# Two small share operations of each expert tile, moved from VectorE to GpSimd

## The chip, the cores and the metric

The kernel runs on one core of one Trainium2 chip. A core has five engines with a queue of instructions each: TensorE (PE; its weight loads are shown as PEld), VectorE (DVE), ScalarE (ACT), GpSimd (POOL), and SyncE (SP), which here only issues DMAs. The engines run side by side and wait for each other by semaphores. The metric is the device time of one execution in microseconds; the lower the better.

## The reference

The input x has 2 batches of 2048 rows of 256. Each row is layer-normalised, and two results are added to it. One is a selective scan along the rows of a batch, taken in an order sorted by cluster. The other is a mixture of 8 experts, of which each row uses its best two:

```python
x = L0_attn_x
xn = _layernorm(x, axis=-1)
x = x + _L0_attn_ref(xn, ...) + _L0_ffn_ref(xn, ...)
...
logits = xt @ w_gate
top_logits, sel = jax.lax.top_k(logits, TOP_K)
probs = jax.nn.softmax(top_logits, axis=-1)
h = jax.nn.silu(xt @ w1[e]) * (xt @ w3[e])
y = h @ w2[e]
out = sum over the two experts of y * probs
```

(The last four lines are written here per expert; the reference computes every expert for every row and then picks.) The share that the change is about is `probs`: the weight with which an expert's result enters a row.

## The kernel before

**The front** (to about 85 us) normalises the rows, chooses clusters and experts, sorts, and writes the normalised rows to DRAM (`xn`). A row there has 256 + 4 numbers. The four behind the row are: the index of its first expert (less 8, column D), the share of its second expert (D+1), the difference of the first share and the second (D+2), and the index of its second expert.

**The expert tiles.** Rows are grouped by expert into 71 tiles of 128 rows; a tile has one expert. `token_of` lists each tile's rows, `w_row` the rows of its weights, `te8` the index of its expert (less 8). A tile t goes through `part_up(t, 0)`, `part_up(t, 1)` and `part_down(t)`:

- `load_rows` (L830): GpSimd gathers the 128 rows from `xn` by an indirect DMA into `xg_sb` (4 buffers).
- `turn` (L839 to L847): TensorE transposes the rows, ScalarE copies them to `xT`, and the two small operations find `own`, one number for each row: (first expert == this tile's expert) x difference + second share. That is the row's share in this tile. `own` has 6 buffers.
- `up` (L856): 32 matmuls by w1 or w3 into PSUM; ScalarE's tanh (L864), VectorE's `silu` (L869) and `gate` (L873).
- `down` (L879): 8 matmuls by w2; ScalarE scales the rows by `own` as it copies them from PSUM into `yo` (L883, 3 buffers); GpSimd adds them to `acc` in DRAM by an indirect DMA (L797), behind the adds before.
- `load_up`, `load_down` (L816): GpSimd fetches the weights of tile t + 3 into the buffers (3 of each) that tile t has just left. Where tile t + 3 has the same expert as tile t, the indices are out of bounds and nothing is moved.

`turn_tile(t)` calls `turn` and then `load_rows` of tile t + 3. It is called in `part_down(t - 2)`, that is two tiles before `own` is used. So in GpSimd's queue a tile's turn of the wheel is: fetch w1/w3, gather rows, add rows, fetch w2.

**The scan** runs in 8 pieces of 512 places, each in 8 steps of four VectorE scans: ScalarE makes `da` (L741), VectorE makes `bu` (L747) and scans `hs` (L756), TensorE transposes `hs` (L768), ScalarE copies to `ht` (L772) and TensorE contracts over the states (L777). GpSimd gathers a piece's rows (`xs`, L601) and adds its results to `acc` (`yt`, L797), four transfers of each per piece.

**The order.** Each engine executes in the order of the text: the last lines of the kernel chain every instruction behind the one before on its engine. The order itself is made when the program is built. Scan steps are laid out place by place, and a job of an expert tile is put in as soon as the sum of the TensorE work given so far falls behind a fixed ratio of VectorE's, by estimates in the code (`PART = 2.05` and `PART_DVE = 0.5` us for a job). These estimates are not touched by the change, so every other instruction keeps its place among those of its engine.

Of the kernel before, what the change touches and what calls it, by code (L numbers as in the profile page):

```python
# [62 lines left out]
def scan_moe_kernel(  # L63
# [14 lines left out]
    nc = tc.nc  # L78
    B, L, D = x.shape
# [527 lines left out]
    class Piece:  # L607
# [9 lines left out]
        def turn(self, h: int):  # L617
            if h == 0:
                self.u = pre.tile([P, ND, CH], F32, tag="tok", name="u")
            pt = ps_m.tile([P, JC, P], F32, tag="m", name="pt_u")  # L620
            for i in range(JC):
                nc.tensor.transpose(pt[:, i, :], self.xs[:, i, h * P : (h + 1) * P], ident)  # L622
            nc.scalar.copy(self.u[:, h, :], pt.rearrange("p i t -> p (i t)"))
# [187 lines left out]
    class Tile:  # L811
# [23 lines left out]
        def turn(self):  # L835
            xg = self.xg
            pt = ps_m.tile([P, ND, P], F32, tag="m", name="pt_g")
            for h in range(ND):
                nc.tensor.transpose(pt[:, h, :], xg[:, h * P : (h + 1) * P], ident)  # L839
            self.xT = ffn.tile([P, ND, TS], F32, tag="xT", name="xT")  # L840
            nc.scalar.copy(self.xT, pt)
            self.own = ffn.tile([P, 1], F32, tag="own", name="own", bufs=6)
            nc.vector.scalar_tensor_tensor(
                self.own, xg[:, D : D + 1], te8[:, self.t : self.t + 1], xg[:, D + 2 : D + 3],
                ALU.is_equal, ALU.mult,
            )
            nc.vector.tensor_add(self.own, self.own, xg[:, D + 1 : D + 2])  # L847

        def up(self, i: int):
            wk = w13_sb[self.t % NW][:, i * ND * H : (i + 1) * ND * H].rearrange(  # L850
# [299 lines left out]
```

## Time and profile before

| what | us |
|---|---|
| median of 3 runs | 818.54 (816.89 to 818.64) |
| the profiled execution | 815.95 |
| its span | 814.1 |
| VectorE busy | 713.9 |
| GpSimd busy | 516.4 |
| ScalarE busy | 504.0 |
| GpSimd's instructions in the span | 374 |

The span is the time from the first to the last profiled instruction. A group row of the profile gives line, engine, operation, what is written <- what is read, shapes and count, then busy us and mean ns, then the idle time of the engine just before these instructions and what ended most of it. A timeline row gives start, duration, and the idle time before in brackets. In the slices each digit is the busy share in tenths of one fortieth of the span (20.4 us).

### The profile page before, as it was taken

The page shows a single profiled execution, that of the slowest core. Times are in us where ns is not written, and L with a number is a line of the kernel's source. Part 1 is how long each engine was busy: PE and PEld are TensorE (multiplying, and loading weights), DVE is VectorE, ACT ScalarE, POOL GpSimd, SP SyncE. Part 2 cuts the span into 40 slices and gives each one's busy share as a digit, 9 for nine tenths or more (in the row PEclk, how much of TensorE's full clock was granted, in tenths as well). Part 3 has the DMA queues.
Part 4 walks back from the last instruction along what each step waited for, and adds up shares of the span by engine and source line. Part 5 has one row for each costly group of instructions (what it writes and reads, how often), then busy time and mean ns, then how long its engine had stood idle before and what let it go on. Part 6 is the DMA issues. An engine that isn't in the chain of part 4 may idle for free.

```text
span 814.1 us, 17139 instructions
## 1 busy us (share of the span) xinstructions
PE 734.4 (90%) x6640; PEld 634.8 (78%) x6640; DVE 713.9 (88%) x1168; ACT 504.0 (62%) x976; POOL 516.4 (63%) x374
## 2 busy tenths in 40 slices
PE   8918697989999999989999999999999998999963
PEld 8914676869987898869877998698869895998842
DVE  8177528989999999989998999899999999799992
ACT  2432136649576866776669666865777667667572
POOL 2002463856786788757877886888758888777413
PEclk8555598999999999999999999999999999999996
DMA  8366343475246845663666458547654775443462
GB/s 266 117 233 187 111 101 129 116 254 154 49 127 171 266 104 167 170 219 86 170 176 204 106 163 253 134 104 234 192 130 99 228 226 119 98 99 95 92 213 26
DMA packets 61216, 125.91 MB, mean 155 GB/s; under 512 B 24464, under 2 KB 42032, under 8 KB 53776
## 3 DMA queue, kind: packets, MB, share of 16 engines
q0 software_dynamic: 40224, 65.03, 33.6%
q1 hardware_dynamic: 20912, 59.80, 21.6%
q8 instruction: 52, 0.85, 0.4%
q14 instruction: 28, 0.23, 0.1%
HBM read 180.06 MB, written 27.00 MB: 254 GB/s over the span
## 4 chain that ended last, share of the span: by engine, by line
PE 67%; ACT 6%; DVE 3%; DMA 2%; issue 2%; POOL 1%; POOLq 0%; SPq 0%; ACTq 0%; DVEq 0%
PE p_ps L856 28%; PE py L879 14%; PE pt_s L768 12%; PE y L777 6%; ACT ht L772 2%; DMA out_dram<-acc 2%; PE y L709 2%; PE pt_g L839 2%; PE px L636 1%; PE pd L673 1%; DVE hs L756 1%; ACT da L741 1%; DVE bu L747 1%; PE px L641 1%; PE pt_u L622 1%
## 5 line engine op out<-in xcount | busy, mean ns | idle before, releaser
L856 PE MATMUL p_ps<-xT,w 128*128 128x128 f32 x2272 | 282.8, 281 | 4.5 <-ACT sq L683 4.3
L856 PEld LDWEIGHTS p_ps<-xT,w 128*128 128x128 f32 x2272 | 271.1, 196 | 19.2 <-issue 9.7
L756 DVE TENSOR_TENSOR_SCAN hs<-da,carry,bu 128x512 f32<-128x512 f32 x192 | 246.3, 1283 | 0.0
L741 ACT ACTIVATE da<-dl,na 128x512 f32<-128x512 f32 x256 | 182.0, 723 | 1.1 <-DVE hs L756 1.0
L747 DVE TENSOR_TENSOR bu<-du,bt 128x512 f32<-128x512 f32 x256 | 174.1, 681 | 0.0
L797 POOL DMA_INDIRECT acc<-yo,token_of x71 | 132.8, 1870 | 64.9 <-ACT yo L883 22.1
L816 POOL DMA_INDIRECT w<-in_w_up_dram,w_row x71 | 93.1, 1312 | 113.6 <-DVE w_row L565 58.6
L772 ACT COPY ht<-pt_s 128x512 f32<-128x512 f32 x256 | 137.2, 590 | 31.4 <-PE pt_s L768 30.9
L768 PE MATMUL pt_s<-ident,hs 128*128 128x128 f32 x1024 | 138.3, 279 | 14.7 <-ACT ht L772 8.7
L879 PE MATMUL py<-w,g 128*128 128x256 f32 x568 | 138.7, 388 | 12.2 <-ACT r L677 8.7
L768 PEld LDWEIGHTS pt_s<-ident,hs 128*128 128x128 f32 x1024 | 118.0, 144 | 31.6 <-ACT ht L772 15.6
L879 PEld LDWEIGHTS py<-w,g 128*128 128x128 f32 x568 | 104.0, 193 | 27.1 <-ACT r L677 10.3
L830 POOL DMA_INDIRECT xg_sb<-xn,token_of x71 | 90.6, 1276 | 34.6 <-issue 15.2
L816 POOL DMA_INDIRECT w<-in_w_down_dram,w_row x71 | 94.2, 1327 | 21.6 <-issue 14.0
L864 ACT ACTIVATE t_sb<-p_ps 128x512 f32<-128x512 f32 x71 | 42.6, 600 | 72.1 <-PE p_ps L856 71.9
L883 ACT ACTIVATE yo<-py,own 128x256 f32<-128x256 f32 x71 | 33.9, 477 | 79.9 <-PE py L879 78.4
L756 DVE TENSOR_TENSOR_SCAN hs<-da,bu 128x512 f32<-128x512 f32 x64 | 78.2, 1222 | 0.0
L777 PE MATMUL y<-ht,z 128*32 128x128 f32 x2048 | 74.3, 279 | 2.6 <-ACT ht L772 1.9
L777 PEld LDWEIGHTS y<-ht,z 128*32 128x32 f32 x2048 | 51.1, 110 | 24.6 <-issue 13.5
L797 POOL DMA_INDIRECT acc<-yt,line_of x28 | 54.1, 1933 | 21.4 <-issue 6.7
L869 DVE SCALAR_TENSOR_TENSOR t_sb<-t_sb,p_ps 128x512 f32<-128x512 f32 x71 | 48.2, 679 | 10.4 <-ACT t_sb L864 10.1
L873 DVE SCALAR_TENSOR_TENSOR g<-t_sb,p_ps 128x512 f32<-128x512 f32 x71 | 48.3, 681 | 7.2 <-PE p_ps L856 4.3
(184 smaller groups left out, 679.2 us busy)
## 6 DMA issues: line engine op xcount, KB each, us to landing
bt<-bc SPq DMA_DIRECT2D x32, 1024.0 KB, 5.2
z<-bc SPq DMA_DIRECT2D x32, 256.0 KB, 3.7
xn<-xt SPq DMA_DIRECT2D x8, 520.0 KB, 4.9
xt<-in_x_dram SPq DMA_DIRECT2D x8, 512.0 KB, 7.2
acc<-in_x_dram SPq DMA_DIRECT2D x8, 512.0 KB, 6.5
w<-in_w_up_dram,w_row POOLq DMA_INDIRECT x71, 6.8
w<-in_w_down_dram,w_row POOLq DMA_INDIRECT x71, 3.8
xg_sb<-xn,token_of POOLq DMA_INDIRECT x71, 3.5
```

Of the source, the lines that this page charges most:

```text
L741: nc.scalar.activation(self.da[i], self.piece.dl[:, self.h, :], AF.Exp, scale=na[:, self.h, n : n + 1])
L747: nc.vector.tensor_mul(self.bu[i], self.piece.du[:, self.h, :], self.piece.bts[self.q][:, i, :])
L756: nc.vector.tensor_tensor_scan(self.hs[:, :, i], self.da[i], self.bu[i], start, ALU.mult, ALU.add)
L768: nc.tensor.transpose(pt[:, j, :], self.hs[:, t0 : t0 + G, :].rearrange("p t n -> p (t n)"), ident)
L772: nc.scalar.copy(self.ht[i], pt)
L777: nc.tensor.matmul(p.ys[self.h][j * G : (j + 1) * G, i, :], lhsT=p.zs[q][:, i * (P // G) + j, :], rhs=self.ht[i][:, j, :], start=False, st ...
L797: ins = nc.gpsimd.indirect_dma_start(out=to, out_offset=bass.IndirectOffsetOnAxis(ap=numbers, axis=0), in_=rows, in_offset=None, compute_o ...
L816: nc.gpsimd.indirect_dma_start(out=to[self.t % NW], out_offset=None, in_=rows, in_offset=bass.IndirectOffsetOnAxis(ap=w_row[:, self.t : se ...
L830: nc.gpsimd.indirect_dma_start(out=self.xg, out_offset=None, in_=xn_d, in_offset=bass.IndirectOffsetOnAxis(ap=token_of[:, self.t : self.t ...
L856: nc.tensor.matmul(p[:, f, :], lhsT=wk[:, h, f * P : (f + 1) * P], rhs=self.xT[:, h, :], start=h == 0, stop=h == ND - 1,)
L873: nc.vector.scalar_tensor_tensor(self.g, self.s, 0.5, self.p3, ALU.mult, ALU.mult)
L879: nc.tensor.matmul(py, lhsT=self.g[:, f, :], rhs=w2[:, f, :], start=f == 0, stop=f == NH - 1)
```

## The change

Both operations are given to GpSimd, as a tensor-by-scalar comparison and product and as an addition. They stand in GpSimd's queue where `turn` is called: after the fetch of w1/w3, ahead of the gather of tile t + 3. The arithmetic is the same.

```diff
             self.own = ffn.tile([P, 1], F32, tag="own", name="own", bufs=6)
-            nc.vector.scalar_tensor_tensor(
+            nc.gpsimd.tensor_scalar(
                 self.own, xg[:, D : D + 1], te8[:, self.t : self.t + 1], xg[:, D + 2 : D + 3],
                 ALU.is_equal, ALU.mult,
             )
-            nc.vector.tensor_add(self.own, self.own, xg[:, D + 1 : D + 2])
+            nc.gpsimd.tensor_add(self.own, self.own, xg[:, D + 1 : D + 2])
```

## The prediction

> **What bounds the kernel now.** I read the page's busy table first, then its slices, then the groups of GpSimd and VectorE in the stretch from 200 to 750 us, then the timeline.
>
> ```profile
> PE 734.4 (90%) x6640; PEld 634.8 (78%) x6640; DVE 713.9 (88%) x1168; ACT 504.0 (62%) x976; POOL 516.4 (63%) x374
> ...
> DVE  8177528989999999989998999899999999799992
> ...
> POOL 2002463856786788757877886888758888777413
> ...
> PE 67%; ACT 6%; DVE 3%; DMA 2%; issue 2%; POOL 1%; POOLq 0%; SPq 0%; ACTq 0%; DVEq 0%
> ```
>
> The chain is put down to TensorE (67%). But between 200 and 750 us, where 58 of the 71 expert tiles run beside the scan, VectorE's digits are 8 and 9, and the sum of its idle gaps there is 22 us of 550: it works back to back, and TensorE works nearly so. GpSimd looks free at 63%. It isn't, and this is the point of the forecast. Its groups from 200 to 750 us (columns: count, busy us and mean ns, then idle before and who ended it):
>
> ```profile
> L797 POOL DMA_INDIRECT acc<-yo,token_of x58 | 109.1, 1882 | 41.7 <-ACT yo L883 9.8 <-ACT da L741 6.2 <-ACT ht L772 5.2
> L816 POOL DMA_INDIRECT w<-in_w_down_dram,w_row x58 | 79.5, 1370 | 17.7 <-issue 11.0 <-PE pt_s L768 2.1 <-PE p_ps L856 1.8
> L816 POOL DMA_INDIRECT w<-in_w_up_dram,w_row x57 | 76.2, 1336 | 25.1 <-issue 7.3 <-PE p_ps L856 6.9 <-PE pt_g L839 5.7
> L830 POOL DMA_INDIRECT xg_sb<-xn,token_of x57 | 75.8, 1330 | 17.4 <-issue 12.2 <-DVE hs L756 1.8 <-DVE bu L747 1.5
> L797 POOL DMA_INDIRECT acc<-yt,line_of x26 | 49.6, 1909 | 20.8 <-issue 6.1 <-ACT ht L772 4.8 <-DMA acc<-yo,token_of 4.7
> L601 POOL DMA_INDIRECT xs<-xn,line_of x24 | 31.2, 1301 | 7.3 <-issue 6.4 <-DMA xs<-xn,line_of 0.6 <-DMA acc<-yo,token_of 0.3
> ```
>
> Busy: 109.1 + 79.5 + 76.2 + 75.8 + 49.6 + 31.2 = 421.4 us in 280 instructions. Idle: 130.0 us. But nearly every gap has a floor of 0.305 us ("issue 0.30" in the timeline, whatever the queue holds), so 280 x 0.305 = 85.4 us of that idle can't be used by another transfer. Real spare time is 130.0 - 85.4 = 44.6 us, or 44.6/57 = 0.78 us per tile. GpSimd is thus 92% taken, and it already runs late: from the timeline, the accumulating DMA of a tile (L797) starts a median 5.3 us and at worst 20.5 us after its rows are ready (L883). The last L856 matmul of a tile frees its up-weight buffer, and the refill (L816) starts a median 5.3 us later.
>
> **What the change removes.** Per tile, two VectorE instructions of 128x1:
>
> ```profile
> L843 DVE SCALAR_TENSOR_TENSOR own<-xg_sb,te 128x1 f32<-128x1 f32 x71 | 15.0, 211 | 0.0
> L847 DVE TENSOR_TENSOR own<-own,xg_sb 128x1 f32<-128x1 f32 x71 | 11.3, 160 | 2.4
> ```
>
> From the start of L843 to the start of what follows is 0.31 us (411.36 to 411.67 in the timeline), so VectorE gets back 71 x 0.31 = 22 us, 58 x 0.31 = 18 us of them in the stretch. TensorE is the other full engine: counted by the start-to-start spacing of each kind (0.11 us for a 128x128 L856 matmul), its matmuls fill some 93% of the stretch, so it can't follow all of that; I take 0.2 us a tile, two thirds, as the gain if nothing else changes: 58 x 0.2 = 12 us. Waits removed: the row gather (L830) waited for VectorE's "own" before it reused a buffer, 0.6 us in 2 places; nothing.
>
> **What it adds on GpSimd.** The order is load of up-weights, [own, own], gather of rows of tile t+3, accumulation of tile t-2, load of down-weights. No transfer is added or leaves its place; all four stand behind the pair. The first own waits for the gather of its rows: issued three tiles before, the time from issue to the transposes that need the same rows is 9.4 us at least (median 19) against a landing of 3.5 us, so that wait is over. (In the lead, tiles 0 and 1 do wait for it, about 3 us, where the queue stood still anyway: 4.3 us before the weight load at 99.6.) The second own waits for the first. ScalarE's yo (L883) now waits for GpSimd; the place where own will stand comes 6.2 us at least before yo (median 14.5), so nothing is late as long as GpSimd doesn't fall further back.
>
> The price of the pair has three terms, none of which the profile shows directly.
>
> (a) The instructions. Nearest rows:
>
> ```profile
> L208 POOL IOTA row_p<- 128x1 f32 x1 | 0.1, 142 | 0.0
> ...
> masks.py:66 POOL TENSOR_SCALAR_AFFINE_SELECT before<-before 128x128 f32<-128x128 f32 x1 | 0.3, 292 | 0.1
> ```
>
> A 128x1 write is 0.14 us; a read of 128 elements with a wait for the writer ahead is 0.29 us after a gap of 0.1. I take 0.2 for each own and 0.1 between: 0.5. Here a rule of the Trainium skill speaks: GPSIMD Engine Reference, "Engine selection", says that GpSimd takes about twice VectorE's time for two-input elementwise work. By it the pair would be 2 x (0.211 + 0.160) = 0.74. At 128x1 the elements hardly count, so I stay near the rows and keep 0.3 to 0.74.
>
> (b) The gaps. The pair puts one to two more hand-overs into the queue: 0 if small instructions follow each other as the iotas do (gap 0.0), 0.5 if each costs a transfer's 0.3. I take 0.15.
>
> (c) The shared port. The timeline around 409 us:
>
> ```profile
> 408.38 1.28 DVE L756 TENSOR_TENSOR_SCAN hs<-da,carry,bu 128x512 f32<-128x512 f32 x1
> 408.99 1.46 POOL L830 DMA_INDIRECT xg_sb<-xn,token_of  x1 [0.31 <-issue]
> 409.58 0.67 DVE L747 TENSOR_TENSOR bu<-du,bt 128x512 f32<-128x512 f32 x1
> ```
>
> This gather takes 1.46 us; beside a VectorE instruction that reads PSUM it takes 0.97 (207.29 us). Its end, 410.45, is 0.79 us after the scan's end at 409.66. All gathers and weight loads follow this: with "wait for the end of a VectorE instruction with two SBUF inputs that began earlier", the predicted excess differs from the recorded one by a median 0.034 us, and the mean excess is 0.36 us. So whatever reads SBUF on GpSimd pays 0.36 us at its turn. The skill's SBUF page (SBUF — State Buffer, "Who interferes with whom") states the same block for a VectorE instruction with two SBUF inputs, but infers that descriptor generation escapes it; the row shows that it doesn't. By the page's inference the transfers' excess would have another cause and the pair alone would wait; by the row both wait, and I put the pair through the recorded VectorE instructions: 0.35 us for the first own, 0.35 for the second (it comes out into the middle of the next one): 0.7 in all. From below: 0.4, if one wait serves both. From above: 1.2, if the second meets a whole scan.
>
> Sum per tile: 0.5 + 0.15 + 0.7 = 1.35; as VectorE is somewhat emptier when GpSimd holds the others back, I take 1.25. Ends: 0.3 + 0 + 0.4 = 0.7 and 0.74 + 0.5 + 1.2 = 2.4.
>
> **The sum.** In the stretch, 57 x 1.25 = 71 us of new work against 44.6 us of spare time: 27 us over. GpSimd may fall back before others notice: a weight load ends a median 15.7 us before its first matmul and needs 6.8 to land, so about 9 us are free: 18 us late. I replayed the queue tile by tile (each transfer with its recorded duration, a start no earlier than its release by TensorE or ScalarE, and everything moved later whenever weights, rows, own or a yo buffer, three of them, came too late). It gives 0 at 0.7 us per tile, +3 at 0.9, +11 at 1.1, +21 at 1.3, +33 at 1.5, +50 at 1.8. With VectorE's 0.2 us per tile taken off: -10, -2, +8, +20, +31, +48. At 1.25 that is +16; stalls of a few us that TensorE's 7% takes up afterwards bring it to +15. The profiled execution took 815.95 us (span 814.1 and 1.9 around it); it becomes 831. The median shown is 818.54, 2.6 above it, so the forecast is 818.5 + 15 = 833.5 us. Before 100 us and after 775 us (the copy to the output) nothing changes.
>
> **The rivals.**
>
> *VectorE's relief wins (faster).* One mechanism: the pair costs under 0.9 us on GpSimd, because own comes between VectorE's instructions without a second wait. At 0.7 us the replay gives -10: 808.5. For it: VectorE is full and TensorE has 7% left. Against: the mean of 0.36 us that each SBUF read pays, twice, leaves 0.2 us for everything else. The turning point is 0.9 to 0.95 us per tile.
>
> *The costs cancel.* Near that point, within 0.2%: 818.5.
>
> *GpSimd becomes much the slowest.* 1.8 to 2.4 us per tile, if each own takes 0.4 us and waits for a scan: +48 to +80, 866 to 898. For it: an access sometimes misses two VectorE instructions in a row (one L797 of 3.12 us against 1.6). Against: the mean.
>
> *VectorE is held by the pair.* 142 reads of at most 0.2 us would take 28 us from it and cancel its relief; a 0.97 us gather delays a neighbour by about 0.05 us (L747 0.72 in place of 0.67), so 7 us. That moves the forecast by under 5 us as long as GpSimd is the bound.
>
> **How the numbers follow.** GpSimd as bound, 0.95 to 1.8 us: 0.70, time 833.5, own range 820 to 864. Much slower: 0.09. Relief wins: 0.17. Cancel: 0.04. 10% off each end gives 809 to 864. A measurement of this kernel can tell about 0.2% from no change. Faster 0.17, same 0.04, slower 0.79.
>
> **What would show it.** Right: GpSimd's "own" rows have means above 0.4 us and many end just after a VectorE scan; gaps of GpSimd above 0.31 us all but vanish between 250 and 700 us; VectorE's idle there grows from 22 us to 35 or more, ended by ScalarE's yo line or by TensorE waiting for weights; L883 and L856 wait for POOL or for a DMA. Wrong: own rows of 0.2 us each without waits and VectorE still back to back (relief), or a GpSimd that keeps its 44 us of slack although the pair is long, which would mean that the transfers get shorter in its company.

## The result and the profile after

The changed kernel takes 882.65 us (median of 4 runs, 878.23 to 886.73) against 818.59 us (816.89 to 818.91, 4 runs): the ratio is 1.0786, 95% interval 1.0714 to 1.0859, that is +64 us. The forecast was +15, in a range that ended at 864. The direction and the engine were right, and the size was wrong by a factor of four. (Now and then an execution of any of these kernels takes some per cent longer; the ratios here and below leave such executions out, the medians don't.)

The profiled execution took 878.23 us, with a span of 876.5 (before: 815.95 and 814.1). From the page of the changed kernel, the busy table, two rows of the slices and the chain:

```profile
PE 760.1 (87%) x6640; PEld 649.8 (74%) x6640; DVE 695.5 (79%) x1026; ACT 503.4 (57%) x976; POOL 643.1 (73%) x516
...
DVE  8186439889979995989979978869699587799981
...
POOL 2003655888888888888878888888888888888732
...
PE 27%; POOL 6%; DMA 5%; issue 5%; ACT 4%; DVE 1%; POOLq 0%; DVEq 0%; ACTq 0%
```

From 150 to 810 us GpSimd's slices are 8, but for one 7 (the gaps of up to 0.3 us keep them from 9), and VectorE's are ragged. Its groups from 200 to 810 us, the stretch that answers to 200 to 750 before:

```profile
L797 POOL DMA_INDIRECT acc<-yo,token_of x57 | 111.2, 1952 | 19.8 <-issue 9.5 <-ACT ht L772 3.4 <-ACT xd L643 1.4
L816 POOL DMA_INDIRECT w<-in_w_up_dram,w_row x58 | 83.7, 1442 | 17.8 <-issue 12.2 <-PE pt_s L768 2.1 <-PE p_ps L856 1.5
L843 POOL TENSOR_SCALAR own<-xg_sb,te 128x1 f32<-128x1 f32 x58 | 77.5, 1335 | 2.8
...
L830 POOL DMA_INDIRECT xg_sb<-xn,token_of x57 | 74.5, 1308 | 8.7 <-issue 5.3 <-DMA acc<-yt,line_of 0.3
...
L847 POOL TENSOR_TENSOR own<-own,xg_sb 128x1 f32<-128x1 f32 x58 | 19.8, 342 | 4.9
```

The compare takes 1.34 us and the addition 0.34. With the hand-overs (2.8/58 = 0.05 ahead, 4.9/58 = 0.08 between, 8.7/57 = 0.15 behind) and less the 0.305 that stood there before, a tile costs GpSimd 1.66 us more. And these are the waits that follow, TensorE's and VectorE's longest in that stretch (total us, times, longest):

```profile
PE pt_u L622 <- DMA xs<-xn,line_of: 19.2, 13, 4.3
PE py L879 <- DMA w<-in_w_down_dram,w_row: 14.3, 5, 6.4
```

```profile
DVE t_sb L869 <- ACT t_sb L864: 64.5, 26, 10.8
DVE g L873 <- PE p_ps L856: 14.6, 12, 4.2
```

TensorE waits for rows and weights that GpSimd fetches too late, and VectorE waits behind TensorE. Neither TensorE wait was there before, and VectorE's two were short:

```profile
DVE t_sb L869 <- ACT t_sb L864: 4.4, 6, 1.9
DVE g L873 <- PE p_ps L856: 1.3, 2, 0.8
```

TensorE does not only wait. Each engine's work from 200 to 750 us, before and after (busy us with the number of instructions of PE, PEld, DVE, ACT and POOL, then the granted clock of TensorE, the DMA share and GB/s):

```profile
200.00:750.00 550.00, 533.48 (x5149) 465.81 (x5148) 529.40 (x767) 383.25 (x751) 420.28 (x280) 0.99 0.58 155
```

```profile
200.00:750.00 550.00, 499.67 (x4585) 426.21 (x4584) 462.57 (x584) 343.75 (x674) 467.15 (x353) 0.95 0.55 146
```

TensorE is idle 50 us in place of 17, and a matmul is busy 0.109 us (499.67/4585) where it was 0.104 (533.48/5149), at a granted clock of 0.95 where it was 0.99. For 5149 matmuls that is some 28 us more (rough, as the ends of matmuls are modelled). I take the slower clock for a companion of the waits and not for a cause beside them: GpSimd hardly ever stands still (next table), and in the changed kernel without the w2 loads (below) the clock is 0.99 again. No run separates the two.

**Where the 62 us between the two spans are.** Count GpSimd's time from its second gather of rows (84.6 us in both) to the start of its last accumulation of a tile (774.7 before, 845.0 after), from the timelines:

| GpSimd, us | before | after | difference |
|---|---|---|---|
| busy | 497.2 | 625.2 | +128.0 |
| of it the pair | 0 | 115.2 | +115.2 |
| gaps, up to 0.31 us of each | 103.3 | 100.6 | -2.7 |
| idle beyond that | 89.5 | 34.6 | -54.9 |
| last accumulation to the end | 39.5 | 31.5 | -8.0 |

Together +62.4. Besides the pair, 12.8 us more are in transfers that took longer. Of the idle time that is left, 26 of 35 us lie before 150 us or after 800 us: in the 650 us between, GpSimd stops for 8 us in all.

### The profile page after: what moved, and what is told of

It is laid out like the page before. It is cut to its first block, busy times and chain, and to the rows that moved or that the text cites. A ratio compares the mean times of both kernels' runs of the same rounds, so it can differ in the third digit from the quotient of the medians.

```text
span 876.5 us, 17108 instructions
## 1 busy us (share of the span) xinstructions
PE 760.1 (87%) x6640; PEld 649.8 (74%) x6640; DVE 695.5 (79%) x1026; ACT 503.4 (57%) x976; POOL 643.1 (73%) x516
## 5 line engine op out<-in xcount | busy, mean ns | idle before, releaser
L856 PE MATMUL p_ps<-xT,w 128*128 128x128 f32 x2272 | 286.0, 283 | 4.8 <-ACT sq L683 4.3
L856 PEld LDWEIGHTS p_ps<-xT,w 128*128 128x128 f32 x2272 | 274.7, 198 | 19.8 <-issue 10.2
L879 PE MATMUL py<-w,g 128*128 128x256 f32 x568 | 146.9, 405 | 31.0 <-DMA w<-in_w_down_dram,w_row 18.5
L816 POOL DMA_INDIRECT w<-in_w_up_dram,w_row x71 | 99.6, 1402 | 96.2 <-DVE w_row L565 58.7
L797 POOL DMA_INDIRECT acc<-yo,token_of x71 | 136.8, 1926 | 33.9 <-issue 10.5
L768 PE MATMUL pt_s<-ident,hs 128*128 128x128 f32 x1024 | 140.7, 282 | 12.7 <-ACT ht L772 8.3
L879 PEld LDWEIGHTS py<-w,g 128*128 128x128 f32 x568 | 108.6, 202 | 49.2 <-issue 10.3
L768 PEld LDWEIGHTS pt_s<-ident,hs 128*128 128x128 f32 x1024 | 120.4, 146 | 30.4 <-ACT ht L772 15.7
L843 POOL TENSOR_SCALAR own<-xg_sb,te 128x1 f32<-128x1 f32 x71 | 92.3, 1300 | 3.4
L777 PE MATMUL y<-ht,z 128*32 128x128 f32 x2048 | 77.6, 287 | 2.7 <-ACT ht L772 2.0
```

Source lines behind the costliest of these rows:

```text
L768: nc.tensor.transpose(pt[:, j, :], self.hs[:, t0 : t0 + G, :].rearrange("p t n -> p (t n)"), ident)
L777: nc.tensor.matmul(p.ys[self.h][j * G : (j + 1) * G, i, :], lhsT=p.zs[q][:, i * (P // G) + j, :], rhs=self.ht[i][:, j, :], start=False, st ...
L797: ins = nc.gpsimd.indirect_dma_start(out=to, out_offset=bass.IndirectOffsetOnAxis(ap=numbers, axis=0), in_=rows, in_offset=None, compute_o ...
L816: nc.gpsimd.indirect_dma_start(out=to[self.t % NW], out_offset=None, in_=rows, in_offset=bass.IndirectOffsetOnAxis(ap=w_row[:, self.t : se ...
L843: nc.gpsimd.tensor_scalar(self.own, xg[:, D : D + 1], te8[:, self.t : self.t + 1], xg[:, D + 2 : D + 3], ALU.is_equal, ALU.mult,)
L856: nc.tensor.matmul(p[:, f, :], lhsT=wk[:, h, f * P : (f + 1) * P], rhs=self.xT[:, h, :], start=h == 0, stop=h == ND - 1,)
```

## The experiments

Times of one and the same kernel differ between chips (the kernel before has medians of 817 to 831 us), so each ratio is taken to runs of the kernel before on the same chip, and kernels from different chips are compared by their ratios.

**The pair twice: VectorE's as before, GpSimd's into a tile that nobody reads.**

```diff
             nc.vector.tensor_add(self.own, self.own, xg[:, D + 1 : D + 2])
+            dum = ffn.tile([P, 1], F32, tag="dum", name="dum", bufs=6)
+            nc.gpsimd.tensor_scalar(dum, xg[:, D : D + 1], te8[:, self.t : self.t + 1],
+                xg[:, D + 2 : D + 3], ALU.is_equal, ALU.mult)
+            nc.gpsimd.tensor_add(dum, dum, xg[:, D + 1 : D + 2])
```

> VectorE finds own as before; GpSimd computes the same two instructions once more into a tile that nobody reads. Theory (GpSimd's queue is the bound; what costs is its time, not who uses the result): as slow as the changed kernel, 875 to 890 us, because the queue carries the same 1.6 us per tile; VectorE's own 22 us don't show. Rival (ScalarE's copy of the rows waits for an own that GpSimd finds too late): nobody waits for the dummy, so 818 to 824 us.

883.88 us, ratio 1.0674 (1.0581 to 1.0767). The result of the pair is wanted by nobody, and the loss is the same within the two intervals (1.0714 to 1.0859 for the change). A late `own` is not the cause; the time on GpSimd's queue is. In the changed kernel too ScalarE waited for `own` only 2.3 us in two places between 200 and 810 us.

**As much time taken off the same queue elsewhere.**

```diff
-            if t + NW < NT:
-                tiles[t + NW].load_down()
```

> The changed kernel without the loads of w2 for tiles 3 to 70 (the down projection then uses stale weights; all else is executed): 68 transfers of 1.36 us and a gap of 0.3, 113 us, taken off GpSimd's queue, about what the pair adds. Theory (GpSimd's queue time is the whole cause): ratio to before 0.99 to 1.01. Rival (late results, or VectorE slowed at the port): 1.04 to 1.08.

> The same loads left out of the kernel before. If GpSimd's lateness cost nothing there, as the prediction had it: 0.995 to 1.002. If it costs something already: 0.97 to 0.99.

819.07 us, ratio 1.0017 (0.9993 to 1.0041), and 817.94 us, 1.0014 (0.9983 to 1.0045). The whole loss is gone, although the pair is still on GpSimd and still waits at the port. Room in the queue is enough to take all of it away. (The run also removes the late w2 weights themselves, 14.3 us of TensorE's waits; but these were late only because the queue was.) This pair of runs settles a second thing. Busy time of each engine from 200 to 750 us, with the instruction counts, of the kernel before without these loads:

```profile
200.00:750.00 550.00, 533.49 (x5141) 465.70 (x5140) 528.77 (x766) 382.80 (x751) 350.38 (x223) 0.99 0.52 138
```

and of the changed kernel without them:

```profile
200.00:750.00 550.00, 533.03 (x5151) 465.06 (x5153) 513.64 (x650) 381.20 (x751) 458.07 (x334) 0.99 0.52 138
```

VectorE is busy 15 us less, and TensorE does the same number of matmuls in the same time (5141 and 5151). VectorE's relief turns into idle time: TensorE, busy 533 of 550 us, sets the pace.

**The pair once more on top of the changed kernel.** The dummy lines above, added to it.

> The changed kernel with the pair once more on GpSimd, into a tile that nobody reads. Theory (GpSimd is the bound everywhere, so that each microsecond per tile costs 68 to 71 us): another 1.5 to 1.6 us per tile, 105 to 112 us: 980 to 1000 us. Rival (part of the loss comes from elsewhere, so that the slope is smaller): 940 to 970.

957.52 us, ratio 1.1559 (1.1483 to 1.1635). By the ratios the second pair brings 0.077, as much as the first (0.079), but less than expected: the time is below the theory's range and inside the rival's, by which a microsecond per tile costs less than 68 to 71 us. The four instructions take 214 us of GpSimd in place of 115, but its transfers take some 15 us less: w1/w3 loads 1.34 us in place of 1.40, w2 loads 1.29 in place of 1.36. VectorE is idle 167 of the 690 us from 200 to 890 by then (94 of the 610 from 200 to 810 with the single pair), so it is likely, though not shown, that what reads SBUF on GpSimd is held up less often.

**One part alone: the addition.**

```diff
-            nc.vector.tensor_add(self.own, self.own, xg[:, D + 1 : D + 2])
+            nc.gpsimd.tensor_add(self.own, self.own, xg[:, D + 1 : D + 2])
```

> One part of the change alone: the compare stays on VectorE, the addition goes to GpSimd. Theory: the addition costs GpSimd 0.2 us and one wait of about 0.4 us, 0.5 us per tile after the saved gap; inside the free 0.78 us. VectorE gets back 0.16 us per tile: 812 to 820 us. Rival (the two share the cost evenly): 0.65 us per tile, 816 to 822. Rival (the result from GpSimd comes late for ScalarE): 830 or more.

837.19 us, ratio 1.0112 (1.0081 to 1.0142). The addition takes 0.48 us and a tile costs GpSimd 0.41 us more, half of the 0.78 that I had called free. It costs 9 us all the same, where I had expected none, and although GpSimd still has 44 us of idle time beyond its gaps from 150 to 800 us (68 before). TensorE's wait for a piece's rows, 0 before, is 8.1 us, and ScalarE waits 8.6 us for `own` (the one-operand compare below costs as much with a result that nobody reads, so this second wait isn't needed for the loss):

```profile
PE pt_u L622 <- DMA xs<-xn,line_of: 8.1, 4, 3.2
```

**The compare alone, and the compare with fewer operands from SBUF.** All go into the dummy tile. The edit shown has three operands; with two, `0.5` stands for `xg[:, D + 2 : D + 3]`, and with one, `-3.0` for `te8` as well.

```diff
+            nc.gpsimd.tensor_scalar(
+                dum, xg[:, D : D + 1], te8[:, self.t : self.t + 1], xg[:, D + 2 : D + 3],
+                ALU.is_equal, ALU.mult,
+            )
```

> As before, with the compare-and-multiply alone on GpSimd into a tile that nobody reads. Theory: 1.28 us and a hand-over per tile, 0.4 us less than the pair, 68 tiles: 27 us less than the changed kernel, 850 to 860 us. Rival (both instructions share the cost evenly, as the prediction had it): 0.65 us per tile, 818 to 822 us.

> The same with one scalar from SBUF and one constant: two SBUF operands. Theory of separate turns: mean 0.8 to 1.0 us, between the other two, ratio 1.015 to 1.028. Rival (only whether there is any scalar from SBUF counts): as with three operands, 1.1 to 1.3 us.

> As before, with one compare-and-multiply on GpSimd whose two scalars are constants in the instruction (one SBUF operand in place of three), into a tile that nobody reads. Theory (each separate SBUF operand of the compare takes its own turn at the port, and each turn can be held by a VectorE instruction): mean 0.5 to 0.7 us against 1.24, and 826 to 834 us on a chip where before takes 820 to 826 (ratio 1.005 to 1.015). Rival (the compare is long by its kind): mean 1.1 to 1.3 us, ratio 1.03 to 1.04 as with the three operands.

Three operands: 856.96 us, ratio 1.0347 (1.0264 to 1.0431). Two: 838.04, 1.0145 (1.0083 to 1.0207). One: 839.29, 1.0134 (1.0087 to 1.0181). Their rows from 200 to 750 us, three, two and one:

```profile
L849 POOL TENSOR_SCALAR dum<-xg_sb,te 128x1 f32<-128x1 f32 x54 | 69.3, 1284 | 2.4
```

```profile
L849 POOL TENSOR_SCALAR dum<-xg_sb,te 128x1 f32<-128x1 f32 x56 | 43.9, 785 | 2.2
```

```profile
L849 POOL TENSOR_SCALAR dum<-xg_sb 128x1 f32<-128x1 f32 x56 | 29.8, 532 | 1.6
```

The same instruction on the same 128 elements takes 1.28, 0.79 or 0.53 us (the 0.79 is just below what was expected). When nothing holds it, the three take 0.38, 0.30 and 0.24 us (the shortest of each run), so the mean wait is 0.90, 0.48 or 0.29 us. It is long by its operands, not by its kind. In time, two operands and one can't be told apart. How the waits come about is seen in the timeline of the changed kernel:

```profile
456.26 2.02 POOL L843 TENSOR_SCALAR own<-xg_sb,te 128x1 f32<-128x1 f32 x1
456.39 0.67 DVE L747 TENSOR_TENSOR bu<-du,bt 128x512 f32<-128x512 f32 x1
456.98 1.28 DVE L756 TENSOR_TENSOR_SCAN hs<-da,carry,bu 128x512 f32<-128x512 f32 x1
458.37 0.19 POOL L847 TENSOR_TENSOR own<-own,xg_sb 128x1 f32<-128x1 f32 x1
```

The compare begins within one scan (455.20 to 456.48), outlives a whole `bu` and ends at 458.28, 0.02 us after the next scan. It is let in between two VectorE instructions and then held again by the next. 19 of the 62 compares between 150 and 800 us take 0.37 to 0.41 us: all but two of them begin where VectorE is idle or works from PSUM. Of the other 43, all but two have such an instruction end within them, a median 0.09 us before their own end, and for 32 of them two or more such instructions ended meanwhile. The addition after it, whose inputs are both tensors, takes 0.19 us in 41 of 61 cases.

**Writing without reading.**

```diff
+            nc.gpsimd.memset(dum, 0.0)
+            nc.gpsimd.memset(dum, 1.0)
```

> As before, with two dependent 128x1 memsets per tile on GpSimd at the place of the pair; they write SBUF and read nothing. Theory (the pair is long because its SBUF reads wait for VectorE's two-input instructions): 0.1 us each and hand-overs that cost about nothing in place of the 0.3 us gap, 0.2 us per tile, inside the 0.78 us that GpSimd has free: 816 to 822 us. Rival (any compute instruction between two indirect transfers costs GpSimd most of a microsecond): 840 us or more.

833.83 us, ratio 1.0061 (1.0016 to 1.0107); slightly above what was expected.

```profile
L830 POOL DMA_INDIRECT xg_sb<-xn,token_of x57 | 74.9, 1315 | 35.4 <-issue 8.1 <-DVE bu L747 7.0 <-DVE hs L756 5.0
...
L849 POOL MEMSET dum<- 128x1 f32 x57 | 7.7, 135 | 0.0
L850 POOL MEMSET dum<- 128x1 f32 x56 | 5.6, 99 | 3.2
```

The writes are not held up (0.14 and 0.10 us). But the gather behind them starts 35.4/57 = 0.62 us later, where behind an `own` it is 0.15, so a tile costs 0.65 us and not 0.2. This is no wait at the port: the gap is 0.60 to 0.67 us in 55 of 63 cases, whether VectorE is idle or not. Nor does it belong to writing: in the run with the dummy pair too the gather starts 0.49 to 0.55 us behind a short addition (0.19 us) in 36 of 37 cases, so that a tile costs 1.79 us there. From start to start that is 0.70 us, and 0.72 behind the second memset; behind the addition of the changed kernel it is 0.34. Why it is longer in these two kernels I haven't found out.

**The share by one instruction.** With share = a + b x expert, a and b found once in the front and stored in the row's spare columns, `own` is one instruction. It was given to ScalarE, as shown, and in two other kernels to VectorE and to GpSimd, as a `tensor_scalar` of `te8` with the two columns (multiply, then add):

```diff
-            nc.vector.scalar_tensor_tensor(
-                self.own, xg[:, D : D + 1], te8[:, self.t : self.t + 1], xg[:, D + 2 : D + 3],
-                ALU.is_equal, ALU.mult,
-            )
-            nc.vector.tensor_add(self.own, self.own, xg[:, D + 1 : D + 2])
+            nc.scalar.activation(self.own, te8[:, self.t : self.t + 1], AF.Identity,
+                bias=xg[:, D + 2 : D + 3], scale=xg[:, D + 1 : D + 2])
```

> The front stores, for each row, a and b such that share = a + b x expert (five small VectorE operations more, once), and ScalarE finds own with one Identity activation; neither VectorE nor GpSimd takes part per tile. It measures what VectorE's relief of 0.31 us per tile is worth when GpSimd isn't charged for it. The prediction's step: 0.2 us per tile, 12 to 14 us: 802 to 808 us. Rival (TensorE sets the pace, the relief is worth nothing): 816 to 821 us. Rival (all of it shows): 796 to 800.

> The same a + b x expert, found on VectorE by one instruction in place of two: VectorE gets back 0.1 to 0.16 us per tile. By the prediction's step of two thirds: 4 to 7 us, 811 to 815 us. If TensorE sets the pace: 818 to 820.

> The same a + b x expert on GpSimd by one instruction with three SBUF operands: GpSimd is charged for the compare's form alone, 1.2 us per tile after the saved gap, and VectorE is relieved of the whole pair. Theory (GpSimd's time per tile sets the end): 845 to 858 us, as with the compare alone. Rival (the handing from the first to the second instruction is what costs): 805 to 820.

ScalarE: 826.26 us, 0.9965 (0.9923 to 1.0008). VectorE: 833.96, 1.0044 (1.0014 to 1.0073). GpSimd: 852.86, 1.0263 (1.0198 to 1.0328). Taking both instructions off VectorE without a charge to GpSimd is worth 0.35% (0.8% at the end of the interval), not the 1.5% that I took, and one instruction of 0.26 us on VectorE in place of two of 0.37 gains nothing; it is 0.4% slower, which is not explained. On GpSimd the single instruction with three operands costs about what the compare did.

**Earlier rows for the scan's pieces.** If the first to be late are these rows, their gather could be placed two steps earlier:

```diff
-            at_place(max(s1 - 1, 0), 1 if n > 1 else 0, p.gather)
+            at_place(max(s1 - 3, 0), 1 if n > 1 else 0, p.gather)
```

> The kernel before, with the gather of a scan piece's rows (L601) two steps (about 16 us) earlier in the order; nothing else. Before, nobody waited for these rows beyond 1.4 us: 0.995 to 1.003 of before.

> The addition alone on GpSimd, and the gather of a piece's rows two steps earlier. Theory (the first to be late behind GpSimd's new work are the piece's rows: TensorE waited 8 us for them with the addition alone, 0 before): the wait of L622 for the rows goes, ratio falls from 1.011 to 0.998 to 1.005. Rival (ScalarE's wait for the addition, L883, is what costs): ratio stays 1.008 to 1.014.

> The changed kernel with the gather of a piece's rows two steps earlier: TensorE's wait of 19 us for these rows goes. Theory of queue time: it comes back as waits for weights and own, ratio 1.07 to 1.085. Rival (the short lead of these rows is a cause of its own): 1.05 to 1.06.

> The share as a + b x expert by one ScalarE activation, and the gather of a piece's rows two steps earlier; GpSimd carries nothing new. The two alone gave 0.9965 and 0.9947: if they add up 0.991, if not 0.994 to 0.998.

Kernel before: 825.75 us, 0.9947 (0.9921 to 0.9973), while the medians of all executions, 825.75 and 827.07, are only 0.2% apart, so that a gain isn't certain. Addition alone: 839.92, 1.0197 (1.0136 to 1.0258) where it was 1.0112. Changed kernel: 897.1, 1.0964 (1.0908 to 1.1020) where it was 1.0786. ScalarE's share and early rows: 819.8, 1.0044 (1.0017 to 1.0071). The last three are slower than any of their expectations. My guess that the rows were a cause of their own fell: with the addition alone TensorE no longer waits for them, but now for weights, 7.9 us for w1/w3 and 3.6 us for w2, which were pushed back; in the changed kernel it waits 18.4 and 25.2 us for these, and ScalarE 57.8 us for `own`. On a full queue an earlier place for one transfer makes the others later. No version was found that is faster than before by more than 0.5%.

The dose, as GpSimd's extra time per tile (from the timeline, tiles after 150 us, hand-overs included) against the ratio: addition 0.41 and 1.011, one-operand compare 0.47 and 1.013, the memsets 0.65 and 1.006, two operands 0.72 and 1.015, three 1.23 and 1.035, the single instruction on GpSimd 1.24 and 1.026, the pair 1.70 (1.66 by the group rows) and 1.079, the dummy pair 1.79 and 1.067, two pairs 3.16 and 1.156. The order is kept roughly, not strictly: time on the queue explains the bulk, and differences of about 1% between kernels stay unexplained.

## Why the prediction was wrong

**What bounds the kernel: right on GpSimd, half right on the rest.** GpSimd at 63% busy was indeed nearly taken, and the loss is its queue. The dummy pair and the kernels without w2 loads show it. VectorE, "back to back", was not what set the pace before: TensorE was, as the chain said.

**The price of the pair: the first step that failed.** I put it at 1.25 us per tile; it is 1.66. Instructions were taken as 0.2 us each: 0.38 and 0.19 when nothing holds them. Port waits were taken as 0.35 each, because a transfer, which reads one index column, pays 0.36. The addition pays less, 0.34 - 0.19 = 0.15; the compare pays 1.34 - 0.38 = 0.96, because it reads three operands from SBUF: with two the same compare waits 0.48, with one 0.29. The hand-overs were mis-sized less: 0.05 + 0.08 + 0.15 - 0.305 is nothing, I took 0.15 and 0.1 between. So term (c) for the compare is 0.6 us short, term (a) 0.2, and the rest partly makes up for it. By the replay, 1.66 in place of 1.25 was worth some 23 us, from 16 to 39: still 23 short of the 62 between the spans.

**The sum: the second step that failed.** Counted as in the table, GpSimd's new work is 128.0 - 2.7 = 125.3 us, where I had 57 x 1.25 = 71.2. Of the 54 us between, 23 are the price (57 x 0.41). Another 18 are the 14 tiles that the sum left out, as if they stood in idle time: over all 71 tiles the pair and its gaps come to 115.2 - 2.7 = 112.5 us, over 57 to 94.6. The last 13 are transfers that took longer, while the replay kept their recorded durations; why they did is open. In the other direction more idle time was used up, 54.9 us in place of 44.6. The 9 us that I let GpSimd end late for free were nearly right: its last accumulation starts 6.9 us after its rows where it was 0.65, but the end comes 8.0 us sooner behind it. With my 17.6 us (71.2 - 44.6 - 9) that gives 17.6 + 54.1 - 10.3 + 1.0 = 62.4, the whole difference of the spans.

The replay had deadlines for weights, rows, own and yo, but not for the scan pieces' rows, which are fetched late in the order. They are the longest of TensorE's new waits, 19.2 us (w2 14.3, and w1/w3, whose deadline the sum was built on, 0.3), and with the addition alone, where the replay said 0, they are already 8.1. Nor did it have matmuls that are busy longer in a stretch in which TensorE is kept waiting (0.109 us in place of 0.104): I had TensorE's free 7% take up stalls.

**The spare time.** 0.78 us per tile was a mean. The addition alone, at 0.41, costs 1.1%; queue time is free only where nobody is due. Leaving the w2 loads out of the kernel before gains nothing (1.0014), so its lateness costs nothing there that shows: GpSimd was at the edge. Whether the earlier gather of the pieces' rows takes 0.5% off the kernel before, and why, stays open.

**VectorE's relief.** I took 12 us of 18. Without the w2 loads it is worth 0 (1.0017 against 1.0014), with ScalarE finding the share 0.35%. The 7% that TensorE seemed to have free by its start-to-start spacing are not to be had that way. At 1.25 us per tile this term made only some 2 us of the forecast, so it is a wrong step, but no large part of the miss.

**The rivals.** "GpSimd becomes much the slowest" (1.8 to 2.4 us per tile, 866 to 898 us), given 0.09, is what happened in time: its mechanism, a second miss at the port, is seen in the timeline. That the time fell into its range is in part luck: the price per tile, 1.66, is below its 1.8 to 2.4, and the terms missing from the sum made up for it. "VectorE is held by the pair" didn't happen: its `bu` takes 0.68 us with and without the pair, its scan 1.28.

**The two rules.** By the doubled time for two-input elementwise work (the Trainium skill, GPSIMD Engine Reference, "Engine selection") the pair's instructions would take 0.74 us; without waits they take 0.57, and with them 1.68. (The rule is for two inputs; the compare on GpSimd has one tensor and two scalars.) Neither the rule nor my rows held the waits, which I added as term (c). That SBUF reads on GpSimd are held by VectorE's two-input instructions (the Trainium skill, SBUF — State Buffer, "Who interferes with whom") is borne out for compute, by 0.96 us on the compare, and so is its statement that instructions that only write escape: the memsets took 0.14 and 0.10 us.

## What to carry to other kernels

A queue of short transfers is as full as its instructions and the gaps between them make it, not as its busy share says; count both, over all tiles up to the last one that the end waits for, and ask of everything that the queue delivers how long its lead is, not only of what the changed instruction stands beside. A small instruction moved to GpSimd next to a VectorE that streams two SBUF inputs cost here by the number of its SBUF operands: the mean wait for VectorE's instructions grew from 0.29 us with one to 0.90 with three. Relief of an engine that is busy all the time is worth next to nothing while another sets its pace: take the engine off the work in one run, without charging another, before counting on it.

## What the runs showed of the hardware

The same 128x1 compare on GpSimd took a mean of 0.53, 0.79 or 1.28 us with one, two or three operands from SBUF, beside a busy VectorE, and 0.24, 0.30 or 0.38 us at the shortest; VectorE's `bu` (0.68 us) and scan (1.28 us) beside it were not longer. The 0.3 us gap between two indirect transfers shrank to 0.15 us behind a compute instruction that reads (8.7/57 in the changed kernel); behind two memsets it was 0.62 us (35.4/57), and behind a short addition of the dummy pair 0.5 us, which is left open. An Identity activation of 128x1 with scale and bias from SBUF took ScalarE 0.40 us; the same operation took VectorE 0.26 us.
